# Two mixtures of experts behind attention and a mixer: where the first mixture's results are kept, and who fetches them

## The chip, the cores and the metric

The kernel runs on one core of one Trainium2 chip, and everything is in 32-bit floats. The metric is device time in microseconds. A core has five engines that run their own instruction streams and meet at semaphores: TensorE (PE; its weight loads are shown apart as PEld), VectorE (DVE), ScalarE (ACT), GpSimd (POOL) and SyncE (SP), which does nothing but issue DMAs. GpSimd issues DMAs too, those whose rows are picked by an index in memory ("indirect").

## The reference, cut to what matters

The input is 2048 tokens of 256 values (8 sequences of 256). Four blocks follow each other, each with a residual sum and a layer norm behind it:

```python
x = layernorm(x + attention(x))        # 16 heads of 128, causal
x = layernorm(x + mixture0(x))         # 32 experts, F 96, top 6, shared F 192
x = layernorm(x + mixer(x))            # a state-space mixer, width 512
x = layernorm(x + mixture1(x))         # 16 experts, F 176, top 4, shared F 352
```

A mixture scores every token against its experts, keeps the top few and their weights, and adds up weighted expert outputs:

```python
act    = silu(x @ wg[e]) * (x @ wu[e])
routed = sum over a token's top experts e of  combine[t, e] * (act @ wd[e])
shared = (silu(x @ sg) * (x @ su)) @ sd
out    = routed + shared
```

So in the first mixture each token has six rows of 256 expert results, which have to be brought together, in the second four.

## The kernel before, in words

**Tiles and groups.** The tokens are 16 tiles of 128, in four groups (`NG`) of four (`GT`). x lives in SBUF (`xg`), a tile is a block of 128 partitions. Attention (lines 1008 to 1047) works through the groups; as a group is done, `layernorm` and `route` (L289) follow for it, woven in as small pieces (`extras`), so routing of groups 0 to 2 lies beside attention and that of group 3 partly behind it.

**Routing.** `route` finds each token's experts and, for each of its picks, a row in a bucket of that expert in DRAM: the buckets are `xs` (`m0xs`, `m1xs`), which hold rows grouped by expert, in tiles of 128 rows of one expert each. A row has 258 words: 256 values of x, the destination of the result (a row number in `m0ys`, L366) and the weight (L369). `xe` collects these rows for a tile of tokens in SBUF, in one of the four buffers of `rowpool`, and GpSimd scatters them, 128 rows per indirect DMA, six per token tile in the first mixture and four in the second (L371). The buckets are blanked first (`blank_buckets`), so that rows of no token have a zero weight and a destination out of bounds.

**Experts.** `Experts.routed` (L612) runs over the tiles of a mixture, software-pipelined in `step`: SP loads a tile of rows (L643, eight tiles ahead in the first mixture, the row number from a table), PE turns it (L506, L510), makes gate and up (L518, ScalarE L523, VectorE L525), turns the hidden values (L534, L536) and multiplies down (L563); ScalarE scales by the row's weight out of PSUM into `ys` (L670, three buffers), and GpSimd scatters the 128 result rows by destination into `m0ys` in DRAM, token by token (L671). The first mixture's loop has 114 tiles (and a branch, L687, for up to 13 more, not taken here); the first 41 can be loaded before group 3 is scattered (`sure`), the others wait for all of its scatters and for a table (`other_tiles`, L417). `Experts.shared` does the shared expert of one group. For group 0 it runs before the loop; for groups 1 to 3 it is taken piece by piece beside the loop (`others`). GpSimd's scatters of group 3 are ordered in turns with the result scatters.

**Combining.** `results` (L690) lets SP load a token tile's six (or four) result rows, 768 KB in the first mixture (512 KB in the second), out of `m0ys`, after all result scatters. `summed` (L747) adds the halves on VectorE (L751), the rest on PE with an identity (L756), and x (L759); `combined` (L737) does it all on VectorE (L741 to L744). `normed` (L716) is the layer norm: statistics on VectorE, the inverse root by a power on GpSimd (L731, L732, L734), the scaling on ScalarE (L735).

**The mixer.** `weave` (L1113) interleaves generators by given shares: `front` (projections and convolutions of a group), `back` (one token tile, in slots), `all_combined` (combine of the first mixture of a group) and `routed_group` (routing of the second mixture). The combine of group 0 comes first, then front(0) with the combine of group 1; in the further slots the fronts and combines of the next groups lie beside the backs. The first update of x by the mixer is L1488 of slot 0. Order on each engine is that of the program.

**The end.** The second mixture runs like the first; then `after1` (L1534) combines its 16 token tiles: seven loads ahead (`AHEAD`), into two pools in turn, `finish` sums, norms and stores a tile (SP, L1549), and after each tile the next load is issued on SP.

Of the kernel before, what the change touches and what calls it, by code (L numbers as in the profile page):

```python
# [12 lines left out]
F32 = mybir.dt.float32  # L13
# [6 lines left out]
P = 128  # L20
# [18 lines left out]
class Moe:  # L39
# [9 lines left out]
    def __init__(self, name, n, f, top, halves, sh, ahead):  # L49
# [36 lines left out]
ROW = DM + 2  # L86
M0 = Moe("m0", E0, F0, TOP0, 1, SH0, 8)
M1 = Moe("m1", E1, F1, TOP1, 2, SH1, 5)
# [10 lines left out]
def kernel(  # L99
# [88 lines left out]
    for m in (M0, M1):  # L188
# [4 lines left out]
        d["xs"] = dram.tile([m.rows, ROW], F32, name=f"{m.name}xs", tag=f"{m.name}xs")  # L193

        d["ys"] = dram.tile([NTOK * m.top, DM], F32, name=f"{m.name}ys", tag=f"{m.name}ys")
# [11 lines left out]
        d["dest"] = new([P, NTOK // P, m.top], "dest", I32)  # L207
        nc.gpsimd.iota(
            d["dest"], pattern=[[P * m.top, NTOK // P], [1, m.top]], base=0,
            channel_multiplier=m.top,  # L210
        )
# [5 lines left out]
    def blank_buckets(m, blank):  # L217

        flat = disp[m.name]["xs"].rearrange("r d -> (r d)")
        many = blank.shape[1]  # L220
        total, step = m.rows * ROW, P * 60 * ROW
        for at in range(0, total, step):
            n = min(step, total - at) // (P * ROW)
            c = many if n % many == 0 else 1
            nc.sync.dma_start(
                flat[at : at + n * P * ROW].rearrange("(p a c) -> p a c", p=P, c=c * ROW),
                blank[:, :c, :].rearrange("p a c -> p (a c)").unsqueeze(1)
                .broadcast_to([P, n // c, c * ROW]),
# [36 lines left out]
    )  # L265

# [22 lines left out]
    def route(m, g, wgate, combine, pool=None):  # L289
# [59 lines left out]
        rows = small.tile([P, top, GT], I32, name=f"{m.name}rows", tag="rows", bufs=2)  # L349
# [8 lines left out]
        for t in range(GT):  # L358

            xe = (pool or rowpool).tile([P, top, ROW], F32, name=f"{m.name}xe{g}_{t}", tag="r")  # L360
            for part in (slice(0, top // 2), slice(top // 2, top)):
# [4 lines left out]
            nc.gpsimd.tensor_copy(  # L366
                xe[:, :, DM : DM + 1].bitcast(I32), d["dest"][:, g * GT + t, :].unsqueeze(2)
            )
            nc.gpsimd.tensor_copy(xe[:, :, DM + 1 :], wts[:, :, t : t + 1])  # L369
            for k in range(top):  # L370
# [4 lines left out]
                )  # L375
                unordered(ins, f"{m.name}xs", d["scatters"])
# [4 lines left out]
                if d["results"]:  # L381
                    tc.add_manual_dep(
                        ins.ins, d["results"][-1].ins.name, NOSYNC, reason="in turns with results"
                    )
# [112 lines left out]
    class Experts:  # L497
# [114 lines left out]
        def routed(self, w, beside=None):  # L612
# [21 lines left out]
            def step(s, lo, hi):  # L634
                i = s + m.ahead
                if i < hi:
# [5 lines left out]
                    xl[i] = self.sb.tile([P, ROW], F32, name=f"{m.name}xl{i}", tag="xl", bufs=m.ahead + 5)  # L642
# [4 lines left out]
                    if part:  # L647

                        tc.declare_no_dep(
# [16 lines left out]
                if lo <= i < hi:  # L666
                    y = self.down(hT.pop(i), wdn, bass.ds(experts[i], 1), f"{m.name}{i}")
                    row = xl.pop(i)
                    ys = self.sb.tile([P, DM], F32, name=f"{m.name}ys{i}", tag="ys", bufs=3)
# [989 lines left out]
```

## Time and profile before

| what | us |
|---|---|
| median of three runs (1579.66 to 1583.66) | 1581.76 |
| profiled execution | 1588.88 |
| its span | 1587.2 |
| PE busy | 1440.3 (91%) |
| DVE busy | 814.7 (51%) |
| ACT busy | 576.9 (36%) |
| POOL busy | 426.5 (27%) |
| first scaling of an expert tile (L670) starts | 731.10 |
| last one of the 114 starts | 968.61 |
| first load of combined rows (L694) starts | 974.29 |
| first update of x by the mixer (L1488) starts | 1079.59 |

The page shows one execution. Its slice rows cut the span in 40 equal parts and give the busy share in tenths; a window row gives the busy time in one stretch; a group row gives a line, engine and operation, out<-in, count, busy time and mean ns, then the engine's idle time before it and what ended it; a row of the timeline is start, duration, engine, line, operation, and in brackets the idle time before it with what released it ("issue": nothing that the profile shows).

### The profile page before, as it was taken

What the parts mean: (1) busy time and instruction counts of PE and PEld (TensorE: products, weight loads), DVE (VectorE), ACT (ScalarE), POOL (GpSimd) and SP (SyncE); (2) the same over time, 40 slices, a digit from 0 to 9 for tenths busy, and PEclk for the clock granted to TensorE, in tenths of its full rate; (3) what the DMA queues carried; (4) which work ended last, traced back from release to release, by engine and by line L of the source; (5) the groups of instructions that cost most, each with busy time, mean ns of one, the idle gap of its engine ahead of it and who ended that gap; (6) DMA issues with size and microseconds to landing.
All of it is one profiled execution on the core that took longest, in us unless ns stands there. A gap on an engine that the chain in (4) does not pass through costs nothing. (4 is left out here: it accounts for less than half of the span.)

```text
span 1587.2 us, 21590 instructions
## 1 busy us (share of the span) xinstructions
PE 1440.3 (91%) x6482; PEld 1020.1 (64%) x6482; DVE 814.7 (51%) x2962; ACT 576.9 (36%) x1498; POOL 426.5 (27%) x600
## 2 busy tenths in 40 slices
PE   8999999999999999997898885898979768999997
PEld 5666665666566666675677773555656557677765
DVE  3444564455544554454354544676666454444436
ACT  3333433334233423351243432556646222233322
POOL 1000005000410031104635554021151442333334
PEclk9999999999999999997999998899989789999999
DMA  9999999800100020162444445310010631233327
GB/s 362 413 413 413 413 409 391 263 1 1 58 24 1 1 90 21 71 210 74 129 142 147 140 146 183 105 66 1 1 54 3 256 124 44 79 106 96 96 81 258
DMA packets 79973, 233.50 MB, mean 147 GB/s; under 512 B 11323, under 2 KB 44378, under 8 KB 78448
## 3 DMA queue, kind: packets, MB, share of 16 engines
q1 hardware_dynamic: 63088, 189.89, 33.7%
q0 software_dynamic: 16768, 42.19, 7.4%
q8 instruction: 56, 0.92, 0.3%
q14 instruction: 61, 0.50, 0.1%
HBM read 80.29 MB, written 155.40 MB: 149 GB/s over the span
## 5 line engine op out<-in xcount | busy, mean ns | idle before, releaser
L933 PE MATMUL qkp<-xT,big 128*128 128x512 f32 x512 | 243.0, 597 | 2.1 <-issue 2.1
L968 ACT ACTIVATE pr<-neg,least 128x128 f32<-128x128 f32 (+1 forms) x256 | 114.4, 449 | 281.8 <-DVE least L963 271.1
L671 POOL DMA_INDIRECT m0ys<-m0ys,m0xl x114 | 112.5, 987 | 99.6 <-ACT m0ys L670 37.3
L933 PEld LDWEIGHTS qkp<-xT,big 128*128 128x128 f32 x512 | 91.1, 191 | 72.5 <-issue 70.4
L941 DVE COPY qk<-qkp 128x512 f32<-128x512 f32 x64 | 44.1, 690 | 178.6 <-PE qkp L933 165.5
L371 POOL DMA_INDIRECT m0xs<-m0xe,m0rows x96 | 92.8, 966 | 154.6 <-DVE pT L984 109.4
L917 PE MATMUL vp<-big,xT 128*128 128x512 f32 x256 | 118.0, 599 | 4.3 <-DVE x L1004 4.3
L999 PE MATMUL op<-big,z 128*128 128x256 f32 x512 | 120.5, 382 | 0.0
L963 DVE CUSTOM_DVE_ANT_0 neg<-sc,cmask 128x128 f32<-128x128 f32 (+1 forms) x256 | 81.3, 354 | 63.9 <-PE sc L953 60.9
L671 POOL DMA_INDIRECT m1ys<-m1ys,m1xl x74 | 72.8, 984 | 115.5 <-ACT m1ys L670 104.3
L999 PEld LDWEIGHTS op<-big,z 128*128 128x128 f32 x512 | 92.6, 190 | 14.9 <-ACT z L1021 4.8
L259 POOL TENSOR_TENSOR rstd<-rstd,numbers 128x1 f32<-128x1 f32 x16 | 8.7, 551 | 305.9 <-DVE rstd L258 305.9
L986 PE MATMUL zp<-pT,big 128*128 128x256 f32 x256 | 77.9, 386 | 2.6 <-issue 2.0
L917 PEld LDWEIGHTS vp<-big,xT 128*128 128x128 f32 x256 | 47.1, 192 | 49.2 <-issue 42.2
L953 PE MATMUL sc<-qk,qk 128*128 128x256 f32 x256 | 77.9, 387 | 0.0
L974 DVE TENSOR_SCALAR pr<-pr,total 128x128 f32<-128x128 f32 (+1 forms) x256 | 70.2, 319 | 3.4
L984 DVE COPY pT<-pt 128x384 f32<-128x384 f32 x128 | 66.9, 549 | 5.9 <-issue 2.2
L986 PEld LDWEIGHTS zp<-pT,big 128*128 128x128 f32 x256 | 48.1, 192 | 33.8 <-issue 14.1
L980 PEld LDWEIGHTS pt<-ident,pr 128*128 128x128 f32 x384 | 47.6, 142 | 33.0 <-issue 30.4
L371 POOL DMA_INDIRECT m1xs<-m1xe,m1rows x64 | 62.1, 970 | 18.7 <-issue 17.0
L949 PEld LDWEIGHTS sc<-qk,qk 128*128 128x128 f32 x256 | 44.2, 193 | 29.6 <-issue 21.1
L980 PE MATMUL pt<-ident,pr 128*128 128x128 f32 x384 | 58.1, 274 | 0.0
(2808 smaller groups left out, 3032.7 us busy)
## 6 DMA issues: line engine op xcount, KB each, us to landing
m0xs<-blank SPq DMA_DIRECT2D x9, 7740.0 KB
m1xs<-blank SPq DMA_DIRECT2D x4, 7740.0 KB
m0xl<-m0xs SPq DMA_DIRECT2D x114, 129.0 KB
m0gy<-m0ys SPq DMA_DIRECT2D x16, 768.0 KB
m1xl<-m1xs SPq DMA_DIRECT2D x74, 129.0 KB
m1gy<-m1ys SPq DMA_DIRECT2D x16, 512.0 KB
big<-in_w_moe SPq DMA_DIRECT2D x1, 5472.0 KB
big<-in_w_heads SPq DMA_DIRECT2D x12, 384.0 KB
```

Of the source, the lines that this page charges most:

```text
L371: ins = nc.gpsimd.indirect_dma_start(out=d["xs"], out_offset=bass.IndirectOffsetOnAxis(ap=rows[:, k, t : t + 1], axis=0), in_=xe[:, k, :], ...
L671: ins = nc.gpsimd.indirect_dma_start(out=d["ys"], out_offset=bass.IndirectOffsetOnAxis(ap=row[:, DM : DM + 1].bitcast(I32), axis=0), in_=y ...
L917: nc.tensor.matmul(ps, lhsT=xT[:, k, t * P : (t + 1) * P], rhs=w_vq[q][:, k, :], start=(k == 0), stop=(k == KC - 1),)
L933: nc.tensor.matmul(ps, lhsT=w_qk[h][:, at : at + P], rhs=xT[:, k, :], start=(k == 0), stop=(k == KC - 1),)
L953: nc.tensor.matmul(sc[:, P:], lhsT=qT[:, c0 + P : c0 + SEQ], rhs=kT[:, c0 : c0 + SEQ], start=True, stop=True,)
L963: nc.vector.tensor_tensor_reduce(out=neg[:, cols], in0=sc[:, cols], in1=cmask[:, cols], scale=-SCALE, scalar=3.0e38, op0=ALU.add, op1=ALU.min,
L968: nc.scalar.activation(pr[:, cols], neg[:, cols], AF.Exp, bias=least[:, i : i + 1], scale=-1.0, accum_out=total[:, i : i + 1],)
L974: nc.vector.tensor_scalar_mul(pr[:, cols], pr[:, cols], total[:, i : i + 1])
L980: nc.tensor.transpose(pt[:, i * P : (i + 1) * P], pr[:, i * P : (i + 1) * P], ident)
L984: pace[0] = nc.vector.tensor_copy(pT, pt)
L986: nc.tensor.matmul(zps[:, b * SEQ : (b + 1) * SEQ], lhsT=vs[2 * b][:, cols], rhs=pT[:, : 2 * P], start=True, stop=False,)
L999: nc.tensor.matmul(ps[:, :DM], lhsT=zs[i][:, t * P : (t + 1) * P], rhs=w_o[q * QH + i], start=(i == 0), stop=(i == QH - 1),)
```

## The change

Eight things are changed.

1. The first mixture's bucket rows have 257 words (`sent` is false: no destination). There is no `m0ys`, no `dest`, and each mixture has a blank of its own width.
2. In its routed loop the scaled result tile (`ys`, four buffers) is written by SP over the first 256 words of the tile's own rows in `m0xs`, in place of the indirect scatter. Loads and writes of `m0xs` are declared independent of each other; loads of the tiles behind `sure` still wait for all scatters.
3. The row numbers of each token's picks are kept in SBUF (`rows0` to `rows3`). `gathered` brings a token tile's six rows by six indirect DMAs of GpSimd, each 128 rows of 257 words, into a `rowpool` buffer; it replaces the loads of 768 KB. The first gather waits for all write-backs.
4. `in_turn` lets at most four of GpSimd's indirect DMAs be under way at once: each waits for the one four before it. It holds for row scatters of both mixtures, the gathers, and the result scatters of the second mixture.
5. The shared experts of groups 1 to 3 of the first mixture leave the routed loop and are woven with the combine of group 0 (weight 18 against 8). The second mixture's shared weights are loaded behind.
6. Row tiles are asked for up to three token tiles at once in groups 0 and 1 and two in groups 2 and 3; the three early loads of `after0` are gone.
7. The norms behind group 0's combine take the inverse root by Newton steps on VectorE (`by_steps`) instead of GpSimd's power.
8. At the end all 16 result loads are issued at once into `big`, where the experts' weights were, and the stores of the output are issued from ScalarE's queue instead of SP's.

```diff
+        self.sent, self.row = sent, DM + 1 + sent
-M0 = Moe("m0", E0, F0, TOP0, 1, SH0, 8)
-M1 = Moe("m1", E1, F1, TOP1, 2, SH1, 5)
+M0 = Moe("m0", E0, F0, TOP0, 1, SH0, False, 8)
+M1 = Moe("m1", E1, F1, TOP1, 2, SH1, True, 5)
...
+    UNDER_WAY = 4
+    sent = []
+
+    def in_turn(ins):
+
+        if len(sent) >= UNDER_WAY:
+            tc.add_manual_dep(
+                ins.ins, sent[-UNDER_WAY].ins.name, SYNC, reason="few at once"
+            )
+        sent.append(ins)
+        return ins
...
+                in_turn(ins)
                 unordered(ins, f"{m.name}xs", d["scatters"])
...
-                if d["results"]:
+                if m.sent and d["results"]:
...
-                    if part:
-
+                    if part or not m.sent:
+
+
+                        tc.add_to_no_dep_group(f"{m.name}xs", ins.ins)
                         tc.declare_no_dep(
...
-                    ys = self.sb.tile([P, DM], F32, name=f"{m.name}ys{i}", tag="ys", bufs=3)
-                    nc.scalar.activation(ys, y, AF.Copy, scale=row[:, DM + 1 :])
-                    ins = nc.gpsimd.indirect_dma_start(
+                    ys = self.sb.tile([P, DM], F32, name=f"{m.name}ys{i}", tag="ys", bufs=3 if m.sent else 4)
+                    nc.scalar.activation(ys, y, AF.Copy, scale=row[:, m.row - 1 :])
+                    ins = nc.sync.dma_start(
+                        d["xs"][bass.ds(rows[i], P), :DM], ys
+                    ) if not m.sent else nc.gpsimd.indirect_dma_start(
...
+    def gathered(m, g, t):
+
+        d = disp[m.name]
+        gy = rowpool.tile([P, m.top, m.row], F32, name=f"{m.name}gy{g}_{t}", tag="r")
+        for k in range(m.top):
+            ins = nc.gpsimd.indirect_dma_start(
+                out=gy[:, k, :], out_offset=None, in_=d["xs"],
+                in_offset=bass.IndirectOffsetOnAxis(ap=d["rows"][g][:, k, t : t + 1], axis=0),
+            )
+            d["first"] = after_all(in_turn(ins), d["first"], d["results"])
+        return gy[:, :, :DM]
...
-        for t in range(3):
-            first[t] = results(M0, 0, t)
-
-    mixture(M0, wsh0, (0,), (1, 2, 3), after0)
+    mixture(M0, wsh0, (0,), (), after0)
...
-                for i in (t, t + 1):
-                    if i < GT and (g, i) not in waits:
-                        waits[g, i] = results(M0, g, i)
+                for i in range(min(t + (3 if g < 2 else 2), GT)):
+                    if (g, i) not in got_rows:
+                        got_rows.add((g, i))
+                        waits[g, i] = gathered(M0, g, i)
                 yield
-                (summed if g < 2 else combined)(M0, g, t, waits.pop((g, t)))
+                (summed if g < 2 else combined)(M0, g, t, waits.pop((g, t)), by_steps=g == 0)
...
-        weave((COMBINE, all_combined(0), 0, 1))
+        def shared_groups():
+            for g in range(1, NG):
+                yield from sh0.shared(g, wsh0)
+
+        weave((COMBINE, all_combined(0), 0, 1), (18, shared_groups(), 0, 1))
...
-        pools = (rowpool, lastrows)
-        AHEAD = 7
+
         rows = {}
-
-        def load(n):
-            if n < len(order):
-                rows[order[n]] = results(M1, *divmod(order[n], GT), pools[n % 2])
+        for n, i in enumerate(order):
+            gy = big[:, n * TOP1 * DM : (n + 1) * TOP1 * DM]
+            rows[i] = results(M1, *divmod(i, GT), gy.rearrange("p (k d) -> p k d", d=DM))
 
         def finish(i, y=None):
             g, t = divmod(i, GT)
             summed(M1, g, t, rows.pop(i), y)
-            nc.sync.dma_start(out_rows[i * P : (i + 1) * P, :], xg[g][:, t, :])
+            nc.scalar.dma_start(out_rows[i * P : (i + 1) * P, :], xg[g][:, t, :])
```

## The prediction

> **What bounds the kernel now.** I read the slice rows of the page first (one slice is 39.7 us), then busy time by stage, then single instructions at the seams.
>
> ```profile
> PE   8999999999999999997898885898979768999997
> POOL 1000005000410031104635554021151442333334
> ```
>
> TensorE is nearly full in attention (slices 1 to 18, to about 703 us) and in the second mixture. The soft part is slices 19 to 34: the first mixture, its combine, the mixer. By stage (window, length, busy us of PE, PE weight load, VectorE, ScalarE, GpSimd, then TensorE's granted clock, DMA share, GB/s):
>
> ```profile
> 703.00:740.00 37.00, 27.01 (x129) 21.98 (x129) 18.32 (x69) 11.84 (x23) 9.95 (x14) 0.86 0.33 105
> 740.00:800.00 60.00, 47.52 (x212) 37.97 (x213) 21.85 (x73) 14.81 (x43) 34.56 (x36) 0.85 0.42 122
> 860.00:920.00 60.00, 53.91 (x326) 46.25 (x325) 30.02 (x107) 23.43 (x70) 35.38 (x36) 1.00 0.46 138
> 975.00:990.00 15.00, 7.89 (x28) 5.90 (x28) 8.56 (x20) 1.20 (x2) 4.49 (x9) 0.74 0.93 336
> 1010.00:1080.00 70.00, 62.89 (x261) 37.68 (x260) 54.15 (x123) 38.52 (x75) 11.76 (x25) 0.95 0.23 79
> 1400.00:1545.00 145.00, 141.67 (x679) 105.44 (x678) 59.88 (x165) 45.38 (x114) 58.47 (x60) 0.99 0.32 93
> ```
>
> At 860 to 920 only M0's routed loop runs, PE is 90% busy and no engine is full. The reason is in the sequence of GpSimd's scatters and ScalarE's scalings:
>
> ```profile
> 867.65 0.98 POOL L671 DMA_INDIRECT m0ys<-m0ys,m0xl  x1 [0.30 <-issue]
> 870.19 0.98 POOL L671 DMA_INDIRECT m0ys<-m0ys,m0xl  x1 [1.56 <-ACT m058s L523]
> 871.48 0.98 POOL L671 DMA_INDIRECT m0ys<-m0ys,m0xl  x1 [0.30 <-issue]
> 872.77 0.98 POOL L671 DMA_INDIRECT m0ys<-m0ys,m0xl  x1 [0.30 <-issue]
> 875.29 0.98 POOL L671 DMA_INDIRECT m0ys<-m0ys,m0xl  x1 [1.54 <-ACT m061s L523]
> ```
> ```profile
> 871.67 0.47 ACT L670 ACTIVATE m0ys<-m055y,m0xl 128x256 f32<-128x256 f32 x1 [0.44 <-DMA m0ys<-m0ys,m0xl]
> 874.55 0.47 ACT L670 ACTIVATE m0ys<-m056y,m0xl 128x256 f32<-128x256 f32 x1 [1.25 <-PE m063xp L506]
> ```
>
> Three scatters, then a wait. `ys` has three buffers; the scatter begun at 870.19 gives its buffer back to the scaling of 874.55, so it holds it 4.36 us (another, 867.65 to 871.67, 4.02). Three tiles per 5.1 us is 1.70 each; scalings of tiles 40 (846.81) and 113 (968.61) give 121.8/73 = 1.67. Undisturbed, PE starts gate-and-up products at 955.06, 956.48, 957.89: 1.415 us a tile. So scatter latency over three buffers costs 0.25 us a tile.
>
> After the loop, PE stands until whole rows have come, all of the core's DMA bandwidth going (0.93, 336 GB/s):
>
> ```profile
> 979.76 4.33 PE L756 MATMUL m0sum<-m0gy,ident 128*128 128x256 f32 x12 [14.39 <-DVE m0gy L751]
> 1079.59 0.48 DVE L1488 SCALAR_TENSOR_TENSOR x<-out,rms,x 128x256 f32<-128x256 f32 x1 [0.98 <-PE out L1484]
> ```
>
> The second row, VectorE's first mixer update of x, is my milestone. In both programs it stands on VectorE behind all of group 3's combine adds, and what follows is the same work. I cost everything up to it, then the tail.
>
> **Part 1, scatters to write-backs in the loop.** Gone: 114 indirect scatters on POOL. Added: 114 plain writes on SP, between loads. SP's dynamic loads start 702.96, 703.55, 704.10 ..., 706.69, 707.21: 0.54 each. If a write costs the same, SP needs 1.08 per tile, under 1.415, so it is hidden; it decides only above 0.87 per write. A write may wait for its scaling with the next load behind it, but loads run eight tiles ahead. With four buffers and the scatter's own 4.4 us a tile could go at 1.1, so PE's 1.415 decides: 73 × 1.415 = 103 instead of 121.8, −18.5. Bounds: 1.415 and the present 1.67.
>
> **Part 2, shared experts of groups 1 to 3 leave the loop.** Tiles 0 to 40 took 731.10 to 846.81, 115.7 us. At PE's pace 40 tiles are 57. PE's shared work is about 8.7 a group from its rows (gate and up 2×2.6, downs 3.5), 26 in all. Two stops, 737 to 743 and 788 to 794, hold all engines (VectorE is idle 6.7 and 7.1); nothing in the change touches what I can see of them, so I keep 13. Group 3's routing and the register loads on PE: 5, an estimate: half of the 10 that 57, 26, 13 and 0.25×40 leave of 115.7 (the other half I take for tiles slowed by the shared products). The load of tile 41 waits for all of group 3's scatters; on SP the write-backs of tiles 31 on are queued behind it, and after four scalings (`ys` buffers) ScalarE stands too: 4 more. 57+13+5+4 = 79: tile 40 at 810, tile 113 at 913 (between 891, without stops, and 930, at the old pace). Group 3's 24 scatters, now not alternating with results, need 24 × 1.27 = 30.5 and are done before 790, earlier than today's 791.8.
>
> **Part 3, gathers for loads.** 16 SP loads of 768 KB go; 96 POOL gathers of 128 rows come. The first waits for the last write: today 969.36 (last scatter) to 974.29 (first load) is 4.9, so it starts at T = 913+0.5+4.9, about 919. No gather is in the trace. The nearest row is the indirect scatter of the same size:
>
> ```profile
> L371 POOL DMA_INDIRECT m0xs<-m0xe,m0rows x96 | 92.8, 966 | 154.6 <-DVE pT L984 109.4
> ```
> ```profile
> 1177.42 0.96 POOL L371 DMA_INDIRECT m1xs<-m1xe,m1rows  x1 [0.30 <-issue]
> 1178.69 0.96 POOL L371 DMA_INDIRECT m1xs<-m1xe,m1rows  x1 [0.30 <-issue]
> ```
>
> 0.97 plus 0.30, a start every 1.27, sixteen in a row. I take 1.27. Lower bound the same (POOL's own cost); upper bound 2.0 (landing 8 us, four under way). Between the gathers stand eight norm triples of 1.12: 9. The last one starts at T + 95×1.27 + 9 = 1049, lands in 4.4, is added in 2.2 (0.95 + 3×0.42), and the milestone follows 2 later: 1057, against 1079.6, −22. The other chain to it: group 0's rows (23×1.27 + 4.4), sum, norm and transposes as from 988.09 to 993.81, then 85.8 of mixer front as before: T + 125 = 1044. POOL's chain is 13 later and decides. Part 2's 26 us of PE lie in the 40 us in which group 0's rows trickle in and PE has only the sums (4.3 + 1.6 + 1.6 today); were that cover missing, 26 would be added. Look-ahead of three tiles fits four row buffers.
>
> Two rules of the Trainium skill bear on it. "SBUF — State Buffer", section "SBUF: two separate sides", says that VectorE, in two-port operations[...], can hold the port that GpSimd needs to write descriptors. That speaks against the change: the combine and the mixer are full of such adds (0.95 for 128x768), and VectorE is 77% busy at 1010 to 1080. If every second gather lost one, 48 × 0.95 = +46. The rows say otherwise: L671 took 0.984 in the loop, L371 0.96 at 1177 with VectorE 50% busy (1165 to 1188). I keep 1.27 and leave +46 to a rival. "DMA: Bandwidth & Descriptors", section "Anatomy of one DMA — SWDGE (gpsimd) path", gives about 2.0 us plus bytes at 436 GB/s: an estimated 2.3 for 132 KB, where the trace shows 4.0 to 4.4. With 2.3 four under way never bind; with 4.4 they allow 1.1; either gives 1.27. They bind above 5.1.
>
> **Part 4, four under way elsewhere.** M1's result scatters come every 2.46 us, four in 9.8, over 4.4; its row scatters at 1.27, four in 5.1. Nothing; the cover in the latter is 0.7 a transfer round, and if landing were 6.4, 0.33 × 64 = 21 would fall on POOL, beside the mixer's PE.
>
> **Parts without price.** Group 0's norms by eleven small VectorE steps of about 0.15: +1.7 per tile in place of POOL, within the trickle (without it they would wait behind gathers). Rows of 257 words, POOL copies gone: attention is PE's. M1's shared weights come later, before a stage with DMA at 0.23.
>
> **Part 5, the end.**
>
> ```profile
> 1562.31 6.17 DMA m1gy<-m1ys
> ```
>
> The chain has one 6.17 wait for rows, whose load stood on SP behind out stores. All 16 loads at once are 8.4 MB, 25 us at 336 GB/s, in a stage with PE 31.4 of 42 busy; some of the 6.17 comes back as waiting for the later rows. Between −7 and +1; I take −4.
>
> **Sum.** −22 − 4 = −26 on a profiled execution of 1588.9 (span 1587.2): 1563. The median of the runs is 7.1 below that execution, so 1581.8 − 26 = 1556.
>
> **Rivals.**
> *Gathers land slowly (slower).* From T to the milestone is 95g + 18; no gain is left when the milestone is at 1083.6 (the end's 4 counted), so g = 1.55, a landing of 6.2. At 7.2 us, g = 1.8: +24, 1606; with the lock of every second gather g = 1.75: +19, 1601. For it: random reads of 1 KB rows are in no row of the trace, VectorE and mixer now run beside. Against: 1.27 in every scatter row.
> *The loop keeps its pace.* SP's writes cost 0.9 or more, or land as late as scatters did: 1.67 a tile, milestone 1076, total −8: 1574.
> *Engines become the bound, gathers hide.* Stops shrink with the freed POOL and tile 113 is at 900: 1543.
> *It only moves work:* if PE's shared work is not covered by the trickle, it goes after the gathers: −26+26, no change.
>
> **How the numbers follow.** Likeliest case 0.52 (1545 to 1568: part 1 and 2's bounds scaled to what POOL's chain passes on), loop pace 0.12, engines 0.07, moved only 0.04, slow gathers 0.25. A measurement here tells 0.3% (5 us) from no change; of the pace case a quarter is within that. Faster 0.52+0.09+0.07 = 0.68; same 0.03+0.04 = 0.07; slower 0.25. The range leaves out the upper half of the slow gathers (0.125) and 0.06 below: 1538 to 1596.
>
> **What would show it.** Right: scalings of M0 1.4 us apart from tile 41 on; last write near 914; gathers 1.27 apart with idle "issue" before them; milestone at 1050 to 1062; PE's shared products between 915 and 960; no 6 us DMA wait after 1540. Wrong: gathers waiting on the DMA of the gather four back, gathers much over 1 us long, SP's queue waiting in the loop, or PE idle again until 1050 as the mixer starves.

## The result and the profile after

The changed kernel takes 1621.83 us (median, 1618.01 to 1632.11), the kernel before 1582.55 (1579.66 to 1583.66): a ratio of 1.0261, 95% interval 1.0227 to 1.0294. It is 39 us slower; 26 us faster was forecast. The profiled execution took 1618.0 with a span of 1615.9 (before 1588.9 and 1587.2).

The slice rows of the page (one slice is now 40.4 us) and busy time by window (length, then busy us of PE, PE weight load, VectorE, ScalarE, GpSimd, then TensorE's granted clock, DMA share, GB/s):

```profile
PE   8999998999899989984899957868997788899997
POOL 2000004000310031105000055473133432533344
```
```profile
740.00:800.00 60.00, 39.10 (x209) 33.39 (x209) 23.00 (x90) 18.80 (x49) 15.22 (x16) 0.76 0.63 162
860.00:920.00 60.00, 58.11 (x368) 52.04 (x367) 35.92 (x123) 29.27 (x82) 0.00 (x0) 1.00 0.82 182
957.00:980.00 23.00, 4.94 (x13) 3.39 (x11) 2.94 (x13) 0.76 (x2) 14.18 (x15) 0.67 0.33 92
980.00:1050.00 70.00, 58.39 (x178) 35.13 (x178) 38.93 (x121) 22.63 (x41) 35.44 (x41) 0.79 0.27 79
1050.00:1115.00 65.00, 50.26 (x201) 29.96 (x200) 40.66 (x90) 27.83 (x56) 41.04 (x54) 0.84 0.25 67
```

The routed loop is what was forecast: at 860 to 920 PE is busy 58.1 of 60 (53.9 before), and GpSimd does nothing. Two places fall short. At 740 to 800 PE has 39.1 where it had 47.5; with the shared products gone 23 tiles are scaled there instead of 18, but the sum had counted on more. And behind the loop there is a long stretch in which no engine is full and 67 to 92 GB/s are moved, where the loads of before had 336. In numbers of single instructions:

| | before | forecast | after |
|---|---|---|---|
| first scaling of an expert tile | 731.10 | as before | 732.92 |
| tile 4 | 745.96 | | 763.49 |
| tile 40 | 846.81 | 810 | 829.26 |
| tile 113, the last | 968.61 | 913 | 933.36 |
| first load, or gather, of combined rows | 974.29 | 919 | 937.97 |
| last gather | | 1049 | 1099.72 |
| front of group 0 starts (`dtp`) | 993.81 | 958 (T + 39) | 1007.93 |
| milestone, the mixer's first update of x | 1079.59 | 1057 | 1114.83 |
| first scaling of the second mixture | 1361.1 | | 1392.93 |
| last one | 1542.04 | | 1573.21 |
| end of the span | 1587.2 | 1561 | 1615.9 |

(The 958 is 1044 less the 85.8 of the front; the 1561 is 1563 less what lies around the span.) All that is lost is lost by the milestone, +35.2, which is +31.2 at the second mixture's last scaling and +28.7 at the end.

The loop's pace in the timeline of ScalarE (start, duration, engine, line, operation; in brackets the idle time before it and what ended it), the queue of SP, the row of the gathers among the page's groups (busy us, mean ns | idle time before them), and how the gathers begin:

```profile
860.40 0.47 ACT L695 ACTIVATE m0ys<-m062y,m0xl 128x256 f32<-128x256 f32 x1 [0.29 <-PE m062y L586]
861.82 0.47 ACT L695 ACTIVATE m0ys<-m063y,m0xl 128x256 f32<-128x256 f32 x1 [0.29 <-PE m063y L586]
```
```profile
875.05 0.36 SPq L696 DMA_DIRECT2D m0xs<-m0ys  x1
875.64 0.33 SPq L666 DMA_DIRECT2D m0xl<-m0xs  x1
```
```profile
L746 POOL DMA_INDIRECT m0gy<-m0xs,m0rows x96 | 94.1, 981 | 237.0 <-SPq L723 178.2
```
```profile
940.56 0.95 POOL L746 DMA_INDIRECT m0gy<-m0xs,m0rows  x1 [0.30 <-issue]
941.82 0.95 POOL L746 DMA_INDIRECT m0gy<-m0xs,m0rows  x1 [0.30 <-issue]
...
1017.20 0.95 POOL L746 DMA_INDIRECT m0gy<-m0xs,m0rows  x1 [10.09 <-PE m0sum L806]
1036.39 1.03 POOL L746 DMA_INDIRECT m0gy<-m0xs,m0rows  x1 [10.81 <-DVE x L794]
```

The tiles go at 1.42, and these scalings wait for PE's product; over the whole loop ten of 114 wait for a buffer that is still being written back, 8.9 us together. A write costs SP 0.36. A gather is 0.98 on GpSimd, and they start 1.26 apart. So far the forecast. But the run of gathers breaks: further on GpSimd stands 10 us twice, for a row buffer that a sum on PE or an add on VectorE still reads. And at 957 to 980 every engine but GpSimd stands (ScalarE's and PE's timeline):

```profile
970.28 0.38 ACT L575 ACTIVATE m0s_0s<-m0s_0gu 128x256 f32<-128x256 f32 x1 [27.02 <-remote]
979.37 0.38 ACT L580 ACTIVATE m0s_1s<-m0s_1gu 64x256 f32<-64x256 f32 x1 [8.70 <-remote]
```
```profile
953.46 1.99 PE L566 MATMUL m0s_0gu<-m0xT,m0ws 128*128 128x256 f32 x8
...
971.18 3.78 PE L566 MATMUL m0s_0gu<-m0xT,m0ws 128*128 128x256 f32 x8 [13.56 <-issue]
```

ScalarE waits until 970.28 for products that PE had finished near 956, by the profile's modelled ends. The semaphore records of the trace say what lies between: PE's counter is not raised between 953.55 and 970.26, then not until 979.35, then five times within 980.07 to 980.28. GpSimd issued gathers 1.25 apart until 975.5, then it stood 4.96 us as well. I call this a stop. The low PE count at 740 to 800 is in part two more of them, beside group 3's 24 scatters, which run from 729.59 to 758.84 without a break (ScalarE):

```profile
747.23 0.25 ACT L546 ACTIVATE m07s<-m07gu 128x96 f32<-128x96 f32 x1 [7.25 <-remote]
...
763.34 0.25 ACT L546 ACTIVATE m08s<-m08gu 128x96 f32<-128x96 f32 x1 [10.04 <-remote]
```

Two kinds of times appear below. In the earlier measurements the kernel before took 1582.6 to 1589.8 us and showed such stops. In the later ones it took 1516.7 to 1517.9, and the longest idle time put down to "remote" or "issue" behind the attention is 3.2 us, of one engine alone. What decides is not known; the chips are numbered on record, and numbers 8 and 15 appear with both kinds, so the chip alone does not seem to. Every ratio is against the kernel before measured beside it; I say "with stops" and "without stops".

### The profile page after: what moved, and what is told of

Its sections match the earlier page's. It is cut to its first block, busy times and chain, and to the rows that moved or that the text cites. A ratio compares the mean times of both kernels' runs of the same rounds, so it can differ in the third digit from the quotient of the medians.

```text
span 1615.9 us, 21766 instructions
## 1 busy us (share of the span) xinstructions
PE 1447.0 (90%) x6482; PEld 1027.2 (64%) x6482; DVE 821.8 (51%) x3009; ACT 579.4 (36%) x1499; POOL 399.2 (25%) x554
## 3 DMA queue, kind: packets, MB, share of 16 engines
q1 hardware_dynamic: 74896, 189.82, 35.2%
## 5 line engine op out<-in xcount | busy, mean ns | idle before, releaser
L746 POOL DMA_INDIRECT m0gy<-m0xs,m0rows x96 | 94.1, 981 | 237.0 <-SPq L723 178.2
L785 ACT ACTIVATE x<-x,off,rstd 128x256 f32<-128x256 f32 x48 | 28.7, 599 | 93.9 <-POOL off L784 60.8
```

What stands on the lines that cost most here:

```text
L746: ins = nc.gpsimd.indirect_dma_start(out=gy[:, k, :], out_offset=None, in_=d["xs"], in_offset=bass.IndirectOffsetOnAxis(ap=d["rows"][g][:, ...
```

## Experiments: the stops

*Fewer under way.* First theory: dense runs of GpSimd's indirect DMAs make the signals late, so a pause after each two should take the stops away. The whole edit of `a_two` and, the other way, of `a_eight`:

```diff
-    UNDER_WAY = 4
+    UNDER_WAY = 2      # a_two; a_eight: 8
```

> The changed kernel with two of GpSimd's transfers under way at once in place of four. Theory (while GpSimd issues indirect DMAs back to back, TensorE's semaphore signals are delivered late, and the other engines stop until the run pauses): with a landing of 4.0 to 4.4 us the starts come 2.0 to 2.2 apart, so the stops at 740 to 763 and 957 to 980 us are gone or under 3 us each, as are those of 8 to 12 us in the second mixture's row scatters; the last gather comes about 96 x 2.1 = 200 us after the first, the milestone (first update of x by the mixer) near 1120 to 1135, and the stage from there to the second mixture is some 20 us shorter; in all 1600 to 1635. Rival (the stops have nothing to do with how dense the indirect DMAs are): stops as long as before, and the slower gathers alone add 80: 1690 or more.

> The changed kernel with eight of GpSimd's transfers allowed under way in place of four. Both theories: at four no gather or scatter waits for the one four back (starts are 1.25 us apart), so nothing changes: 1621 within 6. If four did hold something, 1590 to 1610.

Eight: 1627.24, ratio 1.0274 (1.0227 to 1.0321), as with four; in the changed kernel's profile the waits of gathers for an earlier gather are 0.3 us in all, so four never bound. Two: 1605.21, 1.0124 (1.0075 to 1.0174), 22 us faster than with eight beside it, about half of the loss. The gathers of `a_two` in GpSimd's timeline:

```profile
954.13 0.95 POOL L746 DMA_INDIRECT m0gy<-m0xs,m0rows  x1 [0.92 <-DMA m0gy<-m0xs,m0rows]
955.38 0.94 POOL L746 DMA_INDIRECT m0gy<-m0xs,m0rows  x1 [0.30 <-issue]
957.20 0.94 POOL L746 DMA_INDIRECT m0gy<-m0xs,m0rows  x1 [0.88 <-DMA m0gy<-m0xs,m0rows]
```

Pairs with a pause, 1.8 apart on average, and slower gathers give a faster kernel: the stop at 957 to 980 is gone and the milestone is at 1092.4 instead of 1114.8 (1120 to 1135 was expected). How much of it is the stop is not clear-cut: the wait also shifts the order in which the program is written, see the table below, and two of group 3's combine adds (1101.88 and 1112.31) now stand behind the milestone instead of ahead of it. The stops at the loop's start stay (tile 4 at 765.7), for the scatters of group 3 are 1.27 apart as ever. The next three runs tried to pace those too:

```diff
-                in_turn(ins)
+                in_turn(ins, 2 if m is M0 and g == NG - 1 else UNDER_WAY)   # a_scat2
+                if m is M1 or g == NG - 1:                                   # a_pairs, b_pairs:
+                    in_pairs(ins)     # each third scatter waits for the one before it
```

(`a_pairs` has `UNDER_WAY = 2` besides; `b_pairs` is the kernel before with `in_pairs`.)

> The changed kernel with two under way for the 24 row scatters of the first mixture's group 3 alone, four elsewhere. Theory: the stops between 740 and 763 us (20 us of TensorE) go or fall under 4; the scatters end near 783 in place of 760, tile 40 comes near 805 to 815 in place of 829, tile 113 near 910 to 920, and the whole is 12 to 22 us shorter: 1600 to 1610. Rival (something else at the loop's start stops the engines, as loading of code or weights): the stops stay, 1620 to 1640.

> The changed kernel with two of the gathers under way, and the row scatters of group 3 of the first mixture and of the second mixture in pairs with a pause. Against two under way everywhere (1605), theory: the stops at 740 to 763 and at the second mixture's row scatters (12.5 at 1198 to 1211, 6.7, 4) go too, tile 40 near 812 in place of 830: 1565 to 1588. Rival: no stop goes: 1605 to 1625.

> The kernel before, with one thing of its own: of the row scatters of the first mixture's group 3 and of the second mixture, each third waits until the one before has landed, so they go in pairs with a pause of about 1 us (average start 1.9 apart in place of 1.27). Theory (dense runs of indirect DMAs hold TensorE's signals): the stops at 737 to 743, 788 to 794, 1177 to 1190, 1246 to 1256 and 1293 to 1305 us, together some 45 us, go or fall under 3 each; the runs of 16 scatters take 30 in place of 20, which costs up to 10 at the last group: 1550 to 1572. Rival (the stops come from something else that lies at these places): stops stay, the scatters are only slower: 1582 to 1600.

1620.25, 1.0226 (1.0172 to 1.0281); 1611.53, 1.0150 (1.0119 to 1.0181); 1591.03, 1.0004 (0.9985 to 1.0024). As tests of the theory all three are inconclusive, for the edit did nothing to the row scatters: they still start 1.27 apart (in `b_pairs` group 3's, which alternate with result scatters, 2.58, where it was 2.57). They are declared free of each other, and a wait between two of them has no effect. So the change's own limit of four did not pace row scatters either.

*Real pauses.* A memset on GpSimd that waits for each second scatter is no member of that group, and the scatters behind it wait:

```diff
+        if len(turns) % 2 == 0:
+            stop = nc.gpsimd.memset(mark, 0.0)
+            tc.add_manual_dep(stop.ins, ins.ins.name, SYNC, reason="a pause after each two")
...
+                if m is M1 or g == NG - 1:        # b_pauseM1: m is M1 and g < NG - 1
+                    in_pairs(ins)
```

> In the run of pairs made of the kernel before, the scatters still started 1.27 us apart: the wait on the scatter before was dropped, since both belong to a group declared free of dependencies. Here a small operation of GpSimd waits for each second scatter (of the first mixture's group 3 and of all of the second mixture's) to land, and the next scatter stands behind it; nothing else is changed. Theory (dense runs of indirect DMAs hold TensorE's signals): the stops of 12.8 at 1177 to 1190, 9.8 at 1246 to 1256 and 12.4 at 1293 to 1305 us go or fall under 4; each run of 16 takes some 35 in place of 20: 1560 to 1580, the stop at 737 to 743 also gone. Rival (the stops belong to the places): they stay, 1585 to 1605.

> As the one before, with pauses only in the second mixture's row scatters of groups 0 to 2, not in group 3's of either mixture, whose scatters the loops wait for. Theory: the stops at 1177 to 1190, 1246 to 1256 go, those at 737 to 743 and 788 to 794 stay: 1562 to 1578. Rival: 1585 or more.

> The changed kernel with two gathers under way, and such pauses after each second row scatter of the first mixture's group 3 and of the second mixture. Against two gathers under way alone (1605), theory: the stops at 740 to 763 and those at the second mixture's scatters go too, scatters of group 3 end near 780 to 790, tile 40 comes at 812 to 822 in place of 830: 1570 to 1592. Rival: the stops stay, 1605 to 1630.

> The changed kernel with those pauses between the row scatters alone, gathers as they are (four under way, 1.25 apart). Theory: the stops at 740 to 763 and in the second mixture's scatters go, those at 957 to 980 us stay (17 to 25 us): 1590 to 1608. Rival: 1620 to 1640.

The kernel before has stops as well. One in its mixer (VectorE), and the same scatters of the second mixture's rows in `b_pauseM1` (GpSimd):

```profile
1190.12 0.69 DVE L1331 TENSOR_TENSOR big<-gmp,tri 128x512 f32<-128x512 f32 x1 [12.78 <-remote]
```
```profile
1170.52 0.10 POOL L278 MEMSET mark<- 128x1 f32 x1 [1.12 <-DMA m1xs<-m1xe,m1rows]
1170.79 1.08 POOL L386 DMA_INDIRECT m1xs<-m1xe,m1rows  x1 [0.17 <-issue]
1172.17 0.98 POOL L386 DMA_INDIRECT m1xs<-m1xe,m1rows  x1 [0.30 <-issue]
```

With pauses the stop is gone at each place that has them and stays at each that hasn't: `b_pause` has none above 4 us left behind the attention, but beside the attention, where the scatters of groups 0 to 2 have no pauses, it still has idle times of up to 7.2 us; `b_pauseM1` keeps those of group 3's scatters, `a_pause4` keeps the ones beside the gathers (27.7 us on ScalarE). The time moves less. `b_pause` 1583.52, 0.9989 (0.9964 to 1.0015), where 1580 at most was expected. Its profiled execution is the fastest of its twelve, 1572.5, so the profile cannot say why the median gains nothing; that stays open. `b_pauseM1`, where the scatters have time, 1579.30, 0.9963 (0.9946 to 0.9980): faster than the kernel before. `a_pause2` (two under way besides) 1595.75, 1.0078 (1.0057 to 1.0100); `a_pause4` 1612.11, 1.0172 (1.0120 to 1.0223). The last three are 1 to 4 us over what was expected. In `a_pause2` tile 4 is scaled at 739.5 instead of 763.5, but tile 40 at 826.1 against 829.3: the load of tile 41 has to wait for scatters, the last of which now starts at 807.6 instead of 758.8, the write-backs stand behind it on SP, and ScalarE waits 15.4 us for a buffer at 813.9. So with stops, 0.018 of the ratio's 0.026 goes when scatters and gathers come in pairs, 0.009 of it with `a_pause4`'s pauses beside scatters alone, and a loss of 0.8% is left that these stops don't make (1595.75 is 0.8% above `b_pause` too).

## Experiments: the loop and the end

*Is it only the buffer count?* The kernel before with a fourth `ys` buffer, scatters as they were:

```diff
-  name=f"{m.name}ys{i}", tag="ys", bufs=3)
+  name=f"{m.name}ys{i}", tag="ys", bufs=4 if m is M0 else 3)
```

> The kernel before with four ys buffers in place of three in the first mixture's routed loop, its scatters kept. Rival that the loop is bound by buffers alone: tiles from 40 on 1.42 us apart in place of 1.67, 1563 to 1568. Theory of dense runs: with four buffers GpSimd's scatters come 1.42 apart with gaps of 0.1 to 0.4, TensorE's signals are held there too, and less than half of the 18 us is gained: 1574 to 1590.

1587.69, ratio 1.0000 (0.9980 to 1.0020). Tiles 40 to 113 take 843.41 to 966.07, 1.68 each, as with three buffers. The prediction's arithmetic, a buffer held 4.4 us over three, would give 1.42 with four, so it was not the buffer count; the write-backs on SP do give 1.426. The profile of before says so too: of the 73 scalings after tile 40 only seven wait for a scatter, which has then held its buffer 2.3 to 5.1 us, 3.4 on the mean. The scaling at 874.55, from which the prediction read 4.36, waited for PE. What does set 1.67 is not shown. Between 850 and 960 ScalarE has 11.9 us of idle time put down to nothing, and 12.2 with four buffers (with "remote"); in the loop without stops, below, it has none.

*The end alone* (all 16 loads at once into `big`, stores from ScalarE's queue) in the kernel before:

```diff
-        pools = (rowpool, lastrows)
-        AHEAD = 7
+        for n, i in enumerate(order):
+            gy = big[:, n * TOP1 * DM : (n + 1) * TOP1 * DM]
+            rows[i] = results(M1, *divmod(i, GT), gy=gy.rearrange("p (k d) -> p k d", d=DM))
```

> The kernel before with the end of the change alone (all 16 result loads at once into the expert weights' place, stores from ScalarE's queue). Predicted in the sum as -4 (between -7 and +1): 1576 to 1582. In the changed kernel the stage from the last scaling of the second mixture to the end of the span is 42.7 us against 45.2 before, so 2 to 3.

1587.59 against 1589.84, ratio 0.9987 (0.9974 to 1.0001): a gain of 2, if any.

*The best of both*: the kernel before with the pauses of `b_pauseM1` and this end, measured without stops.

> The kernel before with the pauses of groups 0 to 2 in the second mixture's row scatters (0.9963 of before alone) and the end of the change (0.9987 alone). If the two add up: 0.995, 1576 to 1579.

1517.21, 0.9998 (0.9980 to 1.0015): where there are no stops, the two together gain nothing. So no version here beats the kernel before everywhere; `b_pauseM1` beats it by 0.37% where there are stops.

## Experiments: the shared experts

The changed kernel with the shared experts of groups 1 to 3 back beside the loop (`a_beside`), without them (`a_noshare`), and the kernel before with that move alone (`b_share`):

```diff
-    mixture(M0, wsh0, (0,), (), after0)                                        # a_beside
+    mixture(M0, wsh0, (0,), (1, 2, 3), after0)
-        weave((COMBINE, all_combined(0), 0, 1), (18, shared_groups(), 0, 1))   # a_beside, a_noshare
+        weave((COMBINE, all_combined(0), 0, 1))
```

> The changed kernel with the shared experts of groups 1 to 3 back beside the routed loop. Theory (late signals and the row buffers, not the place of the shared work, lose the time): the loop ends 15 to 26 us later, group 0's combine has less TensorE work exposed to the late signals and is 10 to 25 shorter, in all 1610 to 1635. Rival (moving the shared work is what lost it): 1590 or less.

> The changed kernel without the shared experts of groups 1 to 3 of the first mixture (they are left out). It measures what this work costs where the change puts it. Prediction: hidden in the 40 us in which group 0's rows come, 0 to -6 against the changed kernel. Theory now: TensorE, VectorE and ScalarE take turns on it behind group 0's sums at a granted clock of 0.7 to 0.8, so it lies open: -20 to -40.

> The kernel before with the move of the shared experts of groups 1 to 3 behind the loop alone (scatters and loads as before). The loop is 26 to 30 shorter up to the last scaling. By the prediction's reasoning the combine of group 0 takes 15 us there and covers up to 15 of the 26, so 8 to 12 longer after the loop: -14 to -20 in all. By the theory that the work lies open at a low clock: 25 to 40 longer after the loop, -5 to +12 in all.

`a_beside`, with stops: 1653.04, 1.0424 (1.0377 to 1.0471); 1610 to 1635 was expected, a miss. In the changed kernel the move is a gain of some 26 to 31 us (1653.0 against 1627.2 of `a_eight` beside it, 1621.8 of the changed kernel): without it the loop's last scaling is 22 us later (955.4), and the stage from the first gather to the milestone, 188 us, is not shorter but 11 longer. `a_noshare`, without stops: 1562.17, 1.0311 (1.0277 to 1.0344), against 1.0357 of the changed kernel there: of the 26 us of shared work some 10 are exposed, 16 covered, between the two figures expected. `b_share`: 1524.07, 1.0041 (1.0027 to 1.0054): the move costs 6. From the first to the last scaling its loop takes 194.6 us, against 201.9 in `b_best`, whose loop is that of the kernel before: only 7 us shorter where 26 to 30 was expected, so without stops most of the shared work was already hidden beside the loop. From the first load to the milestone it takes 125.3 instead of 105.4, so with the loads of before there is little cover. In the changed kernel the move is no cause of the loss.

## Experiments: the gathers

*The changed kernel again, without stops* (`a_again`), and one that gathers three of each token's six rows (`a_half`):

```diff
-        for k in range(m.top):
+        for k in range(m.top // 2):      # a_half; the sums take the first half twice
```

> The changed kernel itself once more, beside the kernel before on the chip of this call. The pair before this one ran on a chip where the kernel before takes 1517 in place of 1584 and no stop of over 2 us lies beside dense scatters. If this call's chip is of that kind: theory that the late signals are only part of the loss gives 1.01 to 1.025 of the kernel before, theory that they are all of it 0.985 to 1.00. If it is of the other kind: 1.026 as measured first.

> The changed kernel with three of each token tile's six gathers (the first three rows are added twice, so half of the first mixture's routed sum is left out); the adds, sums and norms stay. Theory (beside the late signals it is GpSimd's chain of 96 gathers, with its waits for row buffers that a later combine frees, that sets the first update by the mixer): 48 gathers are 60 us shorter, the milestone falls from 1115 to 1050 to 1070, where the engines' own chain is, and the whole to 1560 to 1580. Rival (the engines' own work beside the combine, with the shared experts, makes the stage long): the milestone stays above 1095, 1600 or more.

`a_again`: 1572.08 against 1517.90, 1.0357 (1.0335 to 1.0378). No stop is in it (the longest idle time put down to nothing behind the attention is 2.7 us, of ScalarE alone), and the loss is larger, 54 us, which neither theory had. `a_half`: 1551.94 against 1516.68, 1.0231 (1.0202 to 1.0261): half of the gathers are worth 19 us (the milestone is at 1062.1), and 35 are still lost.

Why the loss grows: the loop's gain is mostly gone. Without stops scatters don't hold it: in `b_best`, which scatters from three buffers, tiles 40 to 113 take 810.71 to 915.07, 1.43 each, and in `a_again` 805.09 to 908.52, 1.42. Up to the first gather (913.38) or load (920.88 in `b_best`) the whole change gains 7.5 us, where 55 was forecast. The stage behind it stays as bad: first gather at 913.38, milestone at 1086.41, 173 us; from the first load in the kernel before it is 105.3, and 105.4 in `b_best`.

Where these 173 us go can be read on VectorE. Its timeline in `a_again`, and at the same place in the kernel before:

```profile
953.10 0.96 DVE L801 TENSOR_TENSOR m0gy<-m0gy 128x768 f32<-128x768 f32 x1 [3.13 <-DMA m0gy<-m0xs,m0rows]
...
954.63 0.42 DVE L809 TENSOR_TENSOR x<-x,m0sum 128x256 f32<-128x256 f32 x1 [0.24 <-PE m0sum L806]
...
955.95 0.15 DVE L757 TENSOR_SCALAR newton<-var 128x1 int32<-128x1 int32 x1
960.59 0.96 DVE L801 TENSOR_TENSOR m0gy<-m0gy 128x768 f32<-128x768 f32 x1 [4.48 <-DMA m0gy<-m0xs,m0rows]
961.47 0.15 DVE L758 TENSOR_SCALAR newton<-newton 128x1 int32<-128x1 int32 x1
```
```profile
988.09 0.95 DVE L751 TENSOR_TENSOR m0gy<-m0gy 128x768 f32<-128x768 f32 x1
988.95 0.41 DVE L759 TENSOR_TENSOR x<-x,m0sum 128x256 f32<-128x256 f32 x1
...
990.46 0.96 DVE L751 TENSOR_TENSOR m0gy<-m0gy 128x768 f32<-128x768 f32 x1
992.35 0.96 DVE L751 TENSOR_TENSOR m0gy<-m0gy 128x768 f32<-128x768 f32 x1 [0.93 <-DMA m0gy<-m0ys]
```

The add at 960.59 is that of the sixth tile, group 1's second. It stands between two Newton steps of a norm of group 0, and VectorE waits 4.48 us for its rows; the norm, and the front that needs group 0, wait with it. In both programs seven such adds, four of group 0 and three of group 1, stand on VectorE ahead of the front; group 0's last x (988.95 before, 971.42 in `a_again`) comes behind five of them before, and behind all seven now. Before, that cost little: a tile's rows came in 2 to 3 us (adds at 978.55, 980.44, 983.50, 986.01, 988.09, 990.46, 992.35). Now a tile is six gathers, 7.6 us (922.65, 930.11, 937.86, 945.39, 953.10, 960.59, 968.24). Counted in several profiles:

| | adds ahead of the front | first rows asked for to front | to milestone | VectorE's waits for rows up to the milestone |
|---|---|---|---|---|
| before | 7 | 20 | 105 | 13.1 |
| forecast | 4 (taken) | 39 | 138 | |
| after | 7 | 70 | 177 | 33.2, and the stop |
| `a_two` (gathers 1.8 apart) | 5 | 52 | 154 | 23.6 |
| `a_again` | 7 | 65 | 173 | 45.7 |
| `a_noshare` | 6 | 50 | 168 | 46.2 |
| `a_half` (3 gathers a tile) | 8 | 60 | 156 | 31.3 |
| `a_beside`, with stops | 6 | 72 | 188 | 37.6, and stops |
| `a_rows7` | 9 | 76 | 177 | 55.5 |

For `a_again` the sum closes. To the front: the 42nd gather starts 41 × 1.26 = 52 after the first, its add 3 later, and sums, norms and transposes take the 10 from the seventh add to `dtp`: 65. From there the front of before, 85.8, and what VectorE waits for rows of groups 1 to 3 in between, 4.96 + 3.94 + 6.54 + 5.50 + 1.44 = 22.4, of which the 85.8 holds 3.0 already: 170, measured 173.0. `a_two` has only five adds ahead of the front, and though its gathers are slower, its milestone comes 23 us sooner after the first gather than in the changed kernel; but it has no stop there, and two of group 3's adds moved behind the milestone.

Not every profile closes like this. In `a_noshare` and `a_beside` 117.7 and 116.2 us lie between front and milestone, 18 more than 85.8 and the waits for rows give. And in `a_half` a tile's three gathers take 3.8 us, but the front still comes 60 us after the first: its gathers wait 58.7 us in all for row buffers that sums on PE free late, so halving them does not test the order cleanly.

A second in-order wait lies in the same stretch, and no run tests it. The norms of groups 1 to 3 take their power on GpSimd, in program order among the gathers, and ScalarE stands at the scaling that needs it (GpSimd's and ScalarE's timeline of `a_again`):

```profile
1032.67 0.94 POOL L746 DMA_INDIRECT m0gy<-m0xs,m0rows  x1 [0.30 <-issue]
1033.63 0.26 POOL L781 TENSOR_SCALAR rstd<-mv 128x1 f32<-128x1 f32 x1
```
```profile
1034.85 0.60 ACT L785 ACTIVATE x<-x,off,rstd 128x256 f32<-128x256 f32 x1 [11.00 <-POOL off L784]
```

VectorE had the variance of this norm ready at 1027.9; four more gathers started before the power. From front to milestone ScalarE waits 30.9 us for GpSimd in `a_again`, 3.0 before. What of it reaches the milestone is not known.

*Or is it GpSimd's waits for row buffers?* In `a_again` they are 5.5, 9.2, 10.8 and 3.4 us, and the forecast had a solid run. The last run gives the gathers of group 1 buffers of their own, in mixer scratch that group 0 doesn't use, and issues them right behind group 0's:

```diff
+                if (g, t) == (0, 1):
+                    for i in range(GT):
+                        at = (place["h4"] * SLOT, place["h4"] * SLOT + n, place["e8"] * SLOT, None)[i]
+                        gy = None if at is None else big[:, at : at + n].rearrange("p (k d) -> p k d", d=M0.row)
+                        got_rows.add((1, i))
+                        waits[1, i] = gathered(M0, 1, i, gy)
```

> The changed kernel with three more row buffers for the gathers of group 1 (in mixer scratch that group 0 does not use), its four token tiles gathered right behind group 0's. Theory (part of the 173 us from the first gather to the first mixer update is gathers that wait for a row buffer): the first 48 gathers start 1.25 us apart without a wait for a row buffer, and the milestone comes 10 to 30 us sooner after the first gather than in the changed kernel (177 us on the first chips, 173 on the other), the time falls by as much. Rival (the fronts and combines behind the gathers set the milestone, the waits lie beside them): the waits go and the time moves by less than 5 us. Where TensorE's signals come late beside dense gathers, a longer solid run of them may cost some of the gain back as idle time of all engines put down to nothing.

1570.09 against 1517.49, ratio 1.0365 (1.0319 to 1.0411), where the changed kernel has 1.0357: nothing. The rival is right that the milestone does not move with these waits. They are gone but for one of 4.0 us, the last gather starts at 1044.5 instead of 1071.3, 131.6 after the first (forecast 130), and the milestone is at 1089.7 instead of 1086.4. The time is now spent on VectorE, whose waits for rows have grown from 45.7 to 55.5. The edit also moved the order, nine adds stand ahead of the front instead of seven, so it does not price the buffers alone. PE's timeline shows who waits for the adds, group 0's last x:

```profile
979.60 1.54 PE L1293 MATMUL xTp<-ident,x 128*128 128x128 f32 x6 [7.46 <-DVE x L810]
```

A program with group 1's adds behind group 0's norms, which would test the order directly, was not run. So that the gathers delay the front is measured, and the waits can be read in the timelines; how much the order of the adds costs is worked out from them, not shown by a run of its own.

## Why the prediction was wrong, point by point

**Part 1, right in the number, with stops, and by luck.** 1.426 a tile (forecast 1.415), 17.7 us off these 73 tiles (forecast 18.5). The reason given for the old pace was wrong: a fourth buffer doesn't help, and without stops three buffers are enough for 1.43. The pace of 1.67 was seen only where there are stops, and there the gain was had; without them it is 0.9 us (104.4 in `b_best`, 103.4 in `a_again`).

**Part 2, mis-sized.** 79 was forecast for tiles 0 to 40, 96.3 measured. One failed term is the 13 kept for stops: they come with dense runs of GpSimd's DMAs, and the change makes group 3's 24 scatters one solid run. The first four tiles alone take 30.6, 24.9 over PE's pace. Another is the write-backs. Without stops tiles 0 to 40 take 85.9 (719.16 to 805.09), where the sum without its 13 gives 66, and ScalarE waits 23.9 us there for buffers that are being written back, about half of it while group 3's scatters run (715.92 to 747.32), as at tile 9:

```profile
738.38 0.47 ACT L695 ACTIVATE m0ys<-m09y,m0xl 128x256 f32<-128x256 f32 x1 [4.44 <-DMA m0xs<-m0ys]
```

The prediction had 4 for this, near tile 41. With stops, 19 us of the miss lie ahead of the first gather.

**Part 3, failed, and most of the loss lies here.** The price of a gather was right (1.26 against 1.27). The landing was shorter than taken: 2.9 us from a tile's sixth start to its add, nearer the estimate of 2.3 from the Trainium skill ("DMA: Bandwidth & Descriptors", section "Anatomy of one DMA — SWDGE (gpsimd) path") than the 4.4 taken. No gather shows the lock that the prediction took from the Trainium skill's "SBUF — State Buffer", section "SBUF: two separate sides": 0.98 on the mean and 1.41 at most, with VectorE busy 40.7 of 65 us at 1050 to 1115. Nor does the section count these adds as a hold on descriptors: `tensor_tensor`, which they are, has no two-port mode there and contends with GpSimd's reads alone. The failed step is "the other chain": group 0's rows (23 × 1.27 + 4.4), sum, norm and transposes, then 85.8 of front as before, T + 125. It asked who waits for the rows, and not what stands behind the waiting add on VectorE. The 988.09 that it took for group 0's last add is already the add of group 1's first tile; group 0's fourth is at 986.01, and two more of group 1 follow before the front. With gathers the chain is T + 173 without stops and T + 177 with them: seven tiles' rows ahead of the front and some 22 us of later waits, as worked out above. "Look-ahead of three tiles fits four row buffers" failed as well, with some 30 us of idle GpSimd between the gathers in the changed kernel; but `a_rows7`, with a single such wait of 4.0 us, is not faster. In the profiled execution the chain that was to end at 1044 ended at 1114.8: 19 from the start of the loop, 31 up to the front, 21 behind it.

**The cover of the shared work** was there in part: 16 of 26, measured without stops.

**Part 4, right by luck.** No effect, since the limit doesn't hold where the row scatters are and doesn't bind where the gathers are.

**Part 5, mis-sized:** −2.5 in the profile, −2 in the run of it alone, forecast −4.

**The rivals.** "Gathers land slowly" gives 1606, nearer to the result, but not as it happens: no gather waits much for the one four back (0.3 us in all), and none takes over 1.41 in the changed kernel's profile. Only its place is right. "It only moves work" has a piece of the truth, 10 of its 26 us. What was missing is a rival in which an in-order engine stands at the rows of a tile that nobody needs yet.

## What to carry to other kernels

When a transfer becomes slower but is "started early enough", look at the consumer's engine: every instruction that waits for those rows stops all that stands behind it in program order, so count how many of them stand ahead of the critical work and multiply by the new time per tile. In `a_again` that came within some 3 us; where the transfers also wait for buffers, as in `a_half`, it is too little. The order can be read before anything runs. And idle time that the profile puts down to nothing, in several engines at once, is worth a look at what GpSimd is issuing at that moment.

## What was not expected of the hardware

With stops, PE's semaphore updates come up to 15 us after the modelled end of the products, while GpSimd issues indirect DMAs 1.26 us apart: seen beside row scatters and gathers, in both kernels, with 5 to 29 us of idle time on the waiting engines. Pauses of 1 to 3 us after each two remove them (gathers in `a_two`, scatters in `b_pauseM1`, both in `a_pause2`); result scatters 2.46 us apart cause none. At other times the same kernels, with DMAs as dense, show none. How the one delays the other is not shown. Nor are the 66 us between the two conditions of the kernel before: with the stops behind the attention taken away it still took 1583.5. Part of the difference is there earlier: the first expert tile is scaled at 731.10 with stops and at 713.21 without (`b_best`), and beside the attention's row scatters, which no run paced, the kernel before has idle times of 6.0 to 7.2 us at 265, 422 and 596 put down to "remote". The rest stays open.
